# A graph attention layer and a graph convolution on one core: the first layer's opening sums placed by hand, the diagonal loaded once, the adjacency's side sums re-spaced

## The chip, the core and the metric

The kernel runs on one core of one Trainium2 chip. The metric is device time in microseconds (us): the median of three runs. The engines are named as in the profile: PE is TensorE (its weight loads are PEld), DVE is VectorE, ACT is ScalarE, POOL is GpSimd, SP is SyncE, which here only issues DMAs. DMAs are issued from SP's queue and from ACT's queue.

## What is computed

The reference, cut to what matters (N = 3327 nodes, D = 512 features, float32):

```python
h = relu(layernorm(x))
q, k, v = h @ Wq.T + bq, h @ Wk.T + bk, h @ Wv.T + bv
a = q @ k.T / sqrt(D) + adj + adj
x = x + softmax(a) @ v
h = relu(layernorm(x))
A2 = adj + eye(N)
dscale = diagonal(A2) ** -0.5
temp = A2 @ h @ W.T
x = x + relu((dscale[:, None] * A2 * dscale[None, :]) @ temp)
```

## The kernel before

The nodes are padded to 3328, which are 26 tiles of 128. The work has an opening (weights merged, features normalized and transposed, queries projected), then the scores, then the layers.

**The scores.** Four groups of queries (384 or 448 wide) times thirteen pairs of key tiles are 52 score steps. A score step multiplies blocks by a scheme of seven products in the place of eight (`Chain`, L230, used by `Pair.multiply`, L636). PE writes three kinds of PSUM bank, X, Y and Z, two banks of each; DVE evicts each of them into the tile g, which held the adjacency (L646 for a first product, L654 for a later one); ACT takes the exponential of g (L649, L656); the exponentials P and their side sums, which the same scheme needs later, go to DRAM (pd). For the adjacency the first two of four side sums are made here too, by `sum_of_adjacency` (L621: the add at L628, the diagonal's add at L632), and go to DRAM as sumd. What runs beside the products is listed by hand in `beside_of` (L769): a tuple of seven places, called after the seven evictions of a step. `at_score` holds what is issued ahead of a given score step; `fetch(k + 2)` loads the g tiles of the step after the next (L604).

**The layers.** There are three large products: P times h (g = 0), A2 times the second h (g = 1), A2 times temp (g = 2). Each is split twice by the seven-product scheme. The outer split gives seven block products in the order of `ORDER` (L30: p5, p1, p6, p7, p2, p3, p4), each over two strips s (448 and 384 columns in a matmul), each over six pairs of row tiles and a last single tile. These are 3 x 7 x 2 x 7 = 294 steps, numbered k. A step loads its left block (`left`, L984, called by `Step.load`, tile `part`, issued three steps ahead, five slots), makes four sums on DVE (`four_sums`, L162: one of 896 columns at L164, two of 448 at L165 and L166, made two steps ahead, three slots), and multiplies (`Step.multiply`, seven matmuls at L1036, four at L1027 in the last single step). One matmul leaves two records in the profile. The right blocks (`Right`, L706, tile `b`) are loaded five steps and made three steps ahead, once for both strips; for p6 this takes two further 512-wide operations (L743, L744) and loads of 768 KB a step. After a strip the seven PSUM banks are evicted by `Gather` (L1048).

**Beside the layers.** `Job` (L1119) makes the two missing side sums of A2: it loads a block of sumd and one of the adjacency (L1129, L1130), adds them on DVE two steps later (L1134, the diagonal at L1136), and stores the sum to sumd by ACT's queue a step after that (`post`, L957, and `deliver`). There are 52 jobs. They take their tiles from `job_ring` (L973), four slots, two for a job. In the step `prepare` (L892) stands for, the value weights, their bias and the adjacency's diagonal dg are loaded; `load_diagonal` (L899) loads the diagonal again in a second layout, by_32, with 32 partitions to a block; `prepared` (L909) and `scales` (L905) turn both into dscale. `totals`, `place_totals`, `judge` and `judged` handle the row sums of the softmax.

**What sets the order.** Within the scores the order of DVE, PE, POOL and SP is that in which the code issues (`in_order`, L797), and within the layers that of all five queues (L1470). Across the two the scheduler is free. At L1364 to 1371 the code issues, between the two blocks, the first three steps' loads and the first two steps' sums; the third step's sums are issued in the layers' first step. All of these the scheduler moved up into the last score steps. In the layers, a table `between` maps a step to what is issued in it, loads first and the rest after the step's matmuls; `at(k, what)` enters it.

Of the kernel before, what the change touches and what calls it, by code (L numbers as in the profile page):

```python
# [15 lines left out]
P = 128  # L16
# [19 lines left out]
HALF = 13  # L36
# [11 lines left out]
def graph_layers_kernel(  # L48
# [98 lines left out]
    by_32 = const.tile([P, NP // 32], F32, name="by_32")  # L147

# [460 lines left out]
    class Pair:  # L609
# [26 lines left out]
        def multiply(self, qt):  # L636
# [16 lines left out]
            def more(n, ps):  # L653
                nc.vector.tensor_add(a[n], a[n], ps[:, :wd])  # L654
                if n == 1:
                    nc.scalar.activation(g[0], g[0], AF.Exp)  # L656
                beside[{0: 2, 1: 5, 3: 6}[n]]()
# [103 lines left out]
    pairs = {}  # L761
    fours = mid(12, [P, 2, Q[0]], "s4")
    steps = [(n, t) for n in range(len(groups)) for t in range(HALF)]

    def fetch(k):
        if k < len(steps):
            pairs[k] = Pair(*steps[k])

    def beside_of(k):  # L769
        def on(j, what, *args):  # L770
            if 0 <= j < len(steps):
                getattr(pairs[j], what)(*args)

        def difference():
            if k < len(steps) and steps[k][1] >= 6:
                next(more_of, None)

        return (
            lambda: (on(k - 2, "s4"), on(k - 2, "gather", 0)),
            lambda: (on(k - 1, "s3"), on(k - 2, "gather", 1)),  # L780
            lambda: on(k + 1, "sum_of_adjacency", 0),
            lambda: on(k + 1, "sum_of_adjacency", 1),
            lambda: (on(k - 2, "total", 0), difference()),
            lambda: (on(k - 2, "total", 1), on(k - 1, "s1"), next(ahead, None) if k in making else None),
            lambda: (on(k - 1, "s2"), next(ahead, None) if k in making else None),
        )

    coming = queries(0)
    for ins in more_queries(0, coming):
        if ins:  # L790
            after(ins, parts_made[-1])
    for k in range(2):
        fetch(k)
    for m in range(2):
        pairs[0].sum_of_adjacency(m)
    more_of = iter(())
    with in_order(*(e.engine for e in (nc.vector, nc.tensor, nc.gpsimd, nc.sync))):  # L797
        for k, (n, t) in enumerate(steps):
            for what in at_score.get(k, ()):
                what()  # L800
            if t == 0:
                qt = coming
            fetch(k + 2)
            if t == 2 and n + 1 < len(groups):
                coming = queries(n + 1)
                more_of = more_queries(n + 1, coming)
            beside = beside_of(k)
            pairs[k].multiply(qt)
        k = len(steps)
        beside = beside_of(k)  # L810
        for what in beside[:2]:
            what()
        Chain.finish()
        for what in (*beside[5:], *beside_of(k + 1)[:2]):
            what()
        for _ in ahead:
            pass

    def totals():
        for m in range(2):  # L820
            pairs[len(steps_of_scores) - 1].total(m)
        for s in range(2):
            y0, y1 = (by_32[:, 4 * (STRIPS[s] + y * HT[s]) : 4 * (STRIPS[s] + (y + 1) * HT[s])] for y in range(2))
            nc.vector.tensor_sub(y0, y0, y1)

    def place_totals():
        tiled = job_ring([P, P], "tiled")
        for k in range(P // 32):
            nc.vector.tensor_reduce(tiled[:, 32 * k : 32 * k + 32], ident.rearrange("p (a e) -> p e a", e=32), axis=AX.X, op=ALU.add)
        ps = bank(ROLE["p8"], "tot")[:, : 4 * NT]  # L830
        nc.tensor.matmul(ps, tiled, by_32, start=True, stop=True)
        ps = ps.rearrange("p (i a) -> p i a", a=4)
        for a in range(4):
            nc.scalar.copy(tot[32 * a : 32 * a + 32, :], ps[32 * a : 32 * a + 32, :, a])

    steps_of_scores = steps

    ROLE = {"p1": 0, "p6": 2, "p7": 4, "p5": 6, "p2": 7, "p3": 1, "p4": 5, "p8": 3}  # L840

    def banks_for(*names):
        return {r: bank(ROLE[r], r) for r in names}

    verdict = []

    def judge():

        if N < NP:
            other = small.tile([P, 1], F32, name="other")  # L850
            nc.vector.tensor_sub(other, tot[:, NT - 2 : NT - 1], tot[:, NT - 1 :])
            nc.vector.scalar_tensor_tensor(tot[:, NT - 1 :], other, padding, tot[:, NT - 1 :], op0=ALU.mult, op1=ALU.add)
        within = small.tile([P, NT], F32, name="within")
        nc.vector.tensor_scalar(within, tot, SMALL, None, op0=ALU.is_ge)
        good = small.tile([P, NT], F32, name="good")
        nc.vector.scalar_tensor_tensor(good, tot, LARGE, within, op0=ALU.is_le, op1=ALU.mult)
        most = small.tile([P, 2], F32, name="most")
        nc.vector.tensor_reduce(most[:, 0:1], tot, axis=AX.X, op=ALU.max)
        nc.vector.tensor_reduce(most[:, 1:2], tot, axis=AX.X, op=ALU.min)
        ps = bank(ROLE["p8"], "p8")  # L860
        nc.tensor.matmul(ps[:1, :NT], ones, good, start=True, stop=True)
        for k in range(2):
            nc.tensor.transpose(ps[:1, (k + 1) * P : (k + 2) * P], most[:, k : k + 1], ident)
        verdict.append(ps)

    def judged():
        ps, one = verdict[0], small.tile([1, 4], F32, name="one")
        nc.vector.reduce_sum(one[:, 0:1], ps[:1, :NT], axis=AX.X)
        nc.vector.tensor_reduce(one[:, 1:2], ps[:1, P : 2 * P], axis=AX.X, op=ALU.max)
        nc.vector.tensor_reduce(one[:, 2:3], ps[:1, 2 * P : 3 * P], axis=AX.X, op=ALU.min)  # L870

        nc.vector.scalar_tensor_tensor(one[:, 3:4], one[:, 2:3], RATIO, one[:, 1:2], op0=ALU.mult, op1=ALU.is_ge)
        nc.vector.scalar_tensor_tensor(one[:, 3:4], one[:, 0:1], NT * P - 0.5, one[:, 3:4], op0=ALU.is_ge, op1=ALU.mult)
        nc.vector.tensor_scalar(bad, one[:, 3:4], 0.5, None, op0=ALU.is_lt)

    sd = const.tile([P, NT], F32, name="sd")
    rs = const.tile([P, NT], F32, name="rs")

    def weights(src):

        w = [half(k, [P, 2, D], "w") for k in (12, 13)]
        for c in range(DC):
            nc.sync.dma_start(w[c // 2][:, c % 2], src[c * P : (c + 1) * P])
        return [w[c // 2][:, c % 2] for c in range(DC)]

    LD = adjT.shape[1]
    mh = const.tile([P, NT], F32, name="mh")
    nc.vector.memset(mh, -0.5)
    dg = const.tile([P, NT], F32, name="dg")
    bvs = []  # L890

    def prepare():  # L892
        wv_w1.append(weights(wvT))
        bvs.append(half(11, [P, D], "bv_sb"))
        nc.sync.dma_start(bvs[0], bass.AP(tensor=bv.tensor, offset=bv.offset, ap=[[0, P], [1, D]]))
        with nc.allow_non_contiguous_dma(reason="the diagonal, once"):
            nc.sync.dma_start(dg, bass.AP(tensor=adjT.tensor, offset=adjT.offset, ap=[[LD + 1, P], [P * (LD + 1), NT]]))

    def load_diagonal():  # L899
        with nc.allow_non_contiguous_dma(reason="the diagonal, once"):  # L900
            for a in range(4):
                nc.sync.dma_start(by_32[32 * a : 32 * a + 32], bass.AP(tensor=adjT.tensor, offset=adjT.offset,
                                                                      ap=[[LD + 1, 32], [32 * (LD + 1), 4 * NT]]))

    def scales():  # L905
        nc.vector.tensor_scalar(by_32, by_32, 1.0, None, op0=ALU.add)
        nc.gpsimd.tensor_tensor(by_32, by_32, mhalf.to_broadcast(by_32.shape), op=ALU.pow)

    def prepared():  # L909
        nc.vector.reciprocal(rs, tot)  # L910
        nc.vector.tensor_scalar(dg, dg, 1.0, None, op0=ALU.add)
        nc.gpsimd.tensor_tensor(sd, dg, mh, op=ALU.pow)
        nc.scalar.mul(nsd, sd, -1.0)

    wv_w1 = []

    W, differences = [], []

    def other_weights():

        b11, b21, b22, t1, t2, t3 = blocks((11, 12, 13), "w1")
        b12, t4 = (mid(k, [P, 2, E], "w1") for k in (10, 11))
        W.extend((b11, b12, b21, b22, t1, t2, t3, t4))
        for z in range(2):
            for y in range(2):
                block = w1T[z * E : (z + 1) * E, y * E : (y + 1) * E]
# [3 lines left out]
    def difference():  # L930
        next(differences[0])
# [924 lines left out]
```

## Time and profile before

| what | value |
|---|---|
| three runs | 2151.62, 2150.45, 2151.60 us; median 2151.6 |
| profiled execution, its own time | 2150.57 us |
| its span, from first to last instruction | 2148.6 us |
| granted TensorE clock | 1.0 |
| DMA moved | 592.10 MB, mean 276 GB/s |
| first layer matmul | 608.8 us; the scores end near 622 us |
| packets of q1 (SP) and q10 (ACT) | 75.2% and 7.3% of the 16 DMA engines' span |

A row of the profile's timeline gives the start, the duration, the engine, the line, the operation and its tiles, and in brackets the idle time of the engine just before it and what ended it. A row of the view by stretches gives, for each engine, its busy time within the stretch. A row of the view of waits gives the total, the count and the longest. "Landing" is the time at which a DMA's data has arrived.

### The profile page before, as it was taken

The page shows a single profiled execution, that of the slowest core. Times are in us where ns is not written, and L with a number is a line of the kernel's source. Part 1 is how long each engine was busy: PE and PEld are TensorE (multiplying, and loading weights), DVE is VectorE, ACT ScalarE, POOL GpSimd, SP SyncE. Part 2 cuts the span into 40 slices and gives each one's busy share as a digit, 9 for nine tenths or more (in the row PEclk, how much of TensorE's full clock was granted, in tenths as well). Part 3 has the DMA queues.
Part 4 walks back from the last instruction along what each step waited for, and adds up shares of the span by engine and source line. Part 5 has one row for each costly group of instructions (what it writes and reads, how often), then busy time and mean ns, then how long its engine had stood idle before and what let it go on. Part 6 is the DMA issues. An engine that isn't in the chain of part 4 may idle for free.

```text
span 2148.6 us, 20900 instructions
## 1 busy us (share of the span) xinstructions
PE 2137.7 (99%) x6272; PEld 1181.0 (55%) x6272; DVE 1654.2 (77%) x3235; ACT 273.9 (13%) x441; POOL 69.3 (3%) x63
## 2 busy tenths in 40 slices
PE   9999999999999999999999999999999999999998
PEld 6455555555555555555454555555666665555554
DVE  7479888888997688776777778787466666788888
ACT  6312221112110000001111000000111100000000
POOL 2100000000004000000111000000000000000000
PEclk9999999999999999999999999999999999999999
DMA  8678888888999899888787889986646578978997
GB/s 286 230 250 295 302 309 285 305 293 284 329 330 295 292 367 340 285 298 303 263 307 264 300 282 365 322 315 225 195 157 211 155 210 255 303 225 248 267 284 191
DMA packets 402498, 592.10 MB, mean 276 GB/s; under 512 B 139964, under 2 KB 273480, under 8 KB 402376
## 3 DMA queue, kind: packets, MB, share of 16 engines
q1 hardware_dynamic: 374056, 532.72, 75.2%
q10 hardware_dynamic: 28320, 57.95, 7.3%
q8 instruction: 52, 0.85, 0.2%
q14 instruction: 70, 0.57, 0.1%
HBM read 422.71 MB, written 173.87 MB: 278 GB/s over the span
## 4 chain that ended last, share of the span: by engine, by line
PE 97%; DVE 2%; DMA 1%; issue 0%; ACT 0%; POOL 0%; SPq 0%; DVEq 0%; ACTq 0%
PE p L1036 56%; PE Y L642 13%; PE Z L642 7%; PE p L1027 5%; PE p L1143 4%; PE pw L1204 4%; PE X L642 3%; PE Y L440 2%; PE Z L440 1%; PE mm L482 1%; PE X L440 0%; PE tp L320 0%; DVE part L164 0%; DMA qd<-qs 0%; DMA sum<-o 0%
## 5 line engine op out<-in xcount | busy, mean ns | idle before, releaser
L1036 PE MATMUL p<-part,b 128*128 128x448 f32 (+1 forms) x3528 | 1258.0, 513 | 0.3 <-DVE part L1099 0.2
L1036 PEld LDWEIGHTS p<-part,b 128*128 128x128 f32 x3528 | 669.7, 190 | 541.9 <-issue 289.3
L164 DVE TENSOR_TENSOR part<-part 128x896 f32<-128x896 f32 (+1 forms) x252 | 257.0, 1020 | 67.5 <-PE p L1036 29.9
L642 PE MATMUL Y<-qt,hp 128*128 128x448 f32 (+1 forms) x832 | 308.5, 513 | 0.3 <-DVE g L646 0.2
L642 PEld LDWEIGHTS Y<-qt,hp 128*128 128x128 f32 x832 | 157.7, 190 | 134.2 <-issue 72.8
L642 PE MATMUL Z<-qt,hp 128*128 128x384 f32 (+1 forms) x416 | 162.2, 512 | 0.0
L166 DVE TENSOR_TENSOR part<-part,part 128x448 f32<-128x448 f32 (+1 forms) x219 | 129.5, 591 | 15.3 <-PE p L1036 0.5
L165 DVE TENSOR_TENSOR part<-part,part 128x448 f32<-128x448 f32 (+1 forms) x219 | 129.4, 591 | 7.3
L1027 PE MATMUL p<-part,b 128*128 128x448 f32 (+1 forms) x336 | 124.2, 512 | 0.0
L642 PEld LDWEIGHTS Z<-qt,hp 128*128 128x128 f32 x416 | 79.0, 190 | 66.2 <-issue 37.9
L646 DVE SCALAR_TENSOR_TENSOR g<-g,Y 128x384 f32<-128x384 f32 (+1 forms) x156 | 91.6, 587 | 30.2 <-PE Y L642 26.3
L1079 ACT COPY part<-p 128x384 f32<-128x384 f32 (+1 forms) x33 | 16.6, 503 | 655.2 <-PE p L1036 554.8
L1027 PEld LDWEIGHTS p<-part,b 128*128 128x128 f32 x336 | 63.8, 190 | 54.1 <-issue 31.2
L649 ACT ACTIVATE g<-g 128x768 f32<-128x768 f32 (+1 forms) x48 | 43.0, 896 | 346.5 <-DVE g L646 271.8
L642 PE MATMUL X<-qt,hp 128*128 128x384 f32 (+1 forms) x208 | 81.1, 512 | 0.0
L1080 DVE TENSOR_TENSOR part<-p,part 128x384 f32<-128x384 f32 (+1 forms) x33 | 19.3, 586 | 64.1 <-PE p L1036 63.4
L1143 PE MATMUL p<-w,ct 128*128 128x512 f32 x136 | 61.6, 592 | 0.0
L642 PEld LDWEIGHTS X<-qt,hp 128*128 128x128 f32 x208 | 39.5, 190 | 33.1 <-issue 19.3
L199 POOL TENSOR_TENSOR rstd<-ve,mhalf 128x1 f32<-128x1 f32 x46 | 39.5, 862 | 537.7 <-DVE ve L197 528.7
L1099 DVE TENSOR_TENSOR ct<-p,part 128x448 f32<-128x448 f32 (+1 forms) x72 | 42.3, 609 | 16.1 <-PE p L1027 12.1
L1204 PE MATMUL pw<-w,rows 128*128 128x256 f32 x208 | 53.4, 379 | 0.0
L1134 DVE TENSOR_TENSOR job<-job 128x896 f32<-128x896 f32 (+1 forms) x52 | 53.0, 1019 | 0.0
(193 smaller groups left out, 1682.1 us busy)
## 6 DMA issues: line engine op xcount, KB each, us to landing
part<-sum SPq DMA_DIRECT2D x104, 448.0 KB, 4.6
part<-p SPq DMA_DIRECT2D x91, 448.0 KB, 5.9
part<-sum SPq DMA_DIRECT2D x104, 384.0 KB, 4.0
part<-p SPq DMA_DIRECT2D x91, 384.0 KB, 4.4
part<-in_adjT_dram SPq DMA_DIRECT2D x78, 448.0 KB, 5.0
b<-row SPq DMA_DIRECT2D x234, 128.0 KB, 4.8
part<-in_adjT_dram SPq DMA_DIRECT2D x78, 384.0 KB, 3.8
g<-in_adjT_dram SPq DMA_DIRECT2D x52, 448.0 KB, 4.2
```

Of the source, the lines that this page charges most:

```text
L164: yield nc.vector.tensor_add(o[:, 0:2], g[:, 0:4:3], g[:, 1:2].to_broadcast([P, 2, g.shape[-1]]))
L165: yield nc.vector.tensor_add(o[:, 2], o[:, 1], g[:, 0])
L166: yield nc.vector.tensor_add(o[:, 3], o[:, 2], g[:, 2])
L440: nc.tensor.matmul(ps[:, :w], M[B[name]][:, c, o * P : (o + 1) * P], hp[k][:, A[name], c], start=start and c == 0, stop=c == 1, skip_group ...
L642: nc.tensor.matmul(ps[:, :wd], h_of(self.t, name, k), qt[B[name]][:, k], start=start and k == 0, stop=k == 1, skip_group_check=True)
L646: nc.vector.scalar_tensor_tensor(a[n], a[n], 2.0, ps[:, :wd], op0=ALU.mult, op1=ALU.add if sign > 0 else ALU.subtract)
L649: nc.scalar.activation(g[1], g[1], AF.Exp, **({"bias": pad} if self.t == HALF - 1 else {}))
L1027: yield nc.tensor.matmul(ps[("p2", "p3", "p4", "p8")[k]][:, :w], b[:, z], a[:, 0, y], start=k == 3 and not self.seeded, stop=True, skip_gr ...
L1036: yield nc.tensor.matmul(ps[r][:, :w], b[:, i], m, start=self.t == 0 and not adds, stop=self.t == PAIRS - 1 and r in ("p1", "p5", "p6", "p ...
L1134: nc.vector.tensor_add(self.a, self.a, self.b)
L1143: nc.tensor.matmul(ps, cts[s][y][d][:, k * P : (k + 1) * P], w[d], start=d == 0, stop=d == DC - 1)
L1204: nc.tensor.matmul(ps, a, W[B[name]][:, c], start=new and c == 0, stop=c == 1, skip_group_check=True)
```

## The change

- **Opening sums.** The first three layer steps (now `openers`) are loaded ahead of score steps 44, 45 and 46, within the scores' order. The six adds that make the sums of the first two stand at six named places (`opens`): after the fifth eviction of score steps 47 to 50 (one add each), and after the third and fourth of score step 51. The third step's sums stay where they were issued. `parts`, `view`, `turns`, `left`, `Step` and what they need move up in the file unchanged.
- **The diagonal.** It is loaded once, into dg, by ACT's queue ahead of score step 20, behind the exponential issued last. The loads into by_32, its add and its power are gone; in layer step 12 sixteen copies on ACT write by_32 from dscale in the first layout.
- **Small moves.** The value weights and bias are loaded in step 64 and not in step 2. The identity's tiling on DVE is issued in step 2, its matmul stays in step 3. The matmuls of `judge` go from step 8 to 9, `judged` from 9 to 10.
- **The side sums.** The 52 jobs were three steps apart. Now each step has a weight after the loads of the step five ahead (0.5 in the second strip, 0 to 0.3 in the first, 0 in that of p6), and a job is placed when the weights since the last add up to one, at least two steps apart. The jobs start at steps 7, 9, 12, 16, 18, 20, 22, 31, 33, 35, 39, 44, 46, 48, 51, 54, 58, 60, 62, 64, 67, 70, 73, 75, 77, 81, 86, 88, 90, 92, 99, 102, 104, 106, 109, 112, 115, 117, 119, 128, 130, 132, 134, 141, 144, 146, 148, 151, 154, 157, 159, 161.

```diff
-                    nc.scalar.activation(g[0], g[0], AF.Exp)
+                    Pair.exp = nc.scalar.activation(g[0], g[0], AF.Exp)
...
+    openers = [Step(0, ORDER[0], 0, t, right) for t, right in enumerate(ahead_of)]
+    for n, step in enumerate(openers):
+        at_score.setdefault(44 + n, []).append(step.load)
+
+    def sums_of_openers():
+        for step in openers[:2]:
+            yield from step.sums()
+
+    opens, opening = ((47, 4), (48, 4), (49, 4), (50, 4), (51, 2), (51, 3)), sums_of_openers()
...
+    def load_diagonal():
+        step = adjT.shape[1] + 1
+        with nc.allow_non_contiguous_dma(reason="the diagonal, once"):
+            after(nc.scalar.dma_start(dg, bass.AP(tensor=adjT.tensor, offset=adjT.offset, ap=[[step, P], [P * step, NT]])), Pair.exp)
+
+    at_score.setdefault(20, []).append(load_diagonal)
...
+        def open_up(j):
+            if (k, j) in opens:
+                next(opening)
+
...
-            lambda: on(k + 1, "sum_of_adjacency", 0),
-            lambda: on(k + 1, "sum_of_adjacency", 1),
-            lambda: (on(k - 2, "total", 0), difference()),
+            lambda: (on(k + 1, "sum_of_adjacency", 0), open_up(2)),
+            lambda: (on(k + 1, "sum_of_adjacency", 1), open_up(3)),
+            lambda: (on(k - 2, "total", 0), difference(), open_up(4)),
...
-        with nc.allow_non_contiguous_dma(reason="the diagonal, once"):
-            nc.sync.dma_start(dg, bass.AP(tensor=adjT.tensor, offset=adjT.offset, ap=[[LD + 1, P], [P * (LD + 1), NT]]))
-
-    def load_diagonal():
-        with nc.allow_non_contiguous_dma(reason="the diagonal, once"):
-            for a in range(4):
-                nc.sync.dma_start(by_32[32 * a : 32 * a + 32], bass.AP(tensor=adjT.tensor, offset=adjT.offset,
-                                                                      ap=[[LD + 1, 32], [32 * (LD + 1), 4 * NT]]))
-
-    def scales():
-        nc.vector.tensor_scalar(by_32, by_32, 1.0, None, op0=ALU.add)
-        nc.gpsimd.tensor_tensor(by_32, by_32, mhalf.to_broadcast(by_32.shape), op=ALU.pow)
+
+    def place_scales():
+        for a in range(4):
+            to = by_32[32 * a : 32 * a + 32].rearrange("p (i b) -> p b i", b=4)
+            for b in range(4):
+                nc.scalar.copy(to[:, b], sd[32 * b : 32 * b + 32])
...
-    for n, job in enumerate(jobs):
-        k = k0 + n * (k1 - k0) // len(jobs)
-        at(k, job.load)
-        at(k + 2, job.make)
+
+    def jobs_a_step(k):
+
+        ahead = k + 5
+        r, s = ORDER[ahead // (2 * len(every)) % len(ORDER)], ahead // len(every) % 2
+        if k < number_of(0, 0, 1, 0):
+            return 0.0
+        return 0.5 if s else {"p6": 0.0, "p1": 0.3, "p2": 0.3, "p3": 0.3}.get(r, 0.15)
+
+    due, total, placed = 0.0, sum(jobs_a_step(k) for k in range(k0, k1)), []
+    for k in range(k0, k1):
+        due += jobs_a_step(k) * len(jobs) / total
+        if due > 1e-6 and len(placed) < len(jobs) and (not placed or k > placed[-1] + 1):
+            job = jobs[len(placed)]
+            at(k, job.load)
+            at(k + 2, job.make)
+            placed, due = placed + [k], due - 1.0
+    assert len(placed) == len(jobs)
...
-    for k, what in ((1, totals), (3, place_totals), (2, prepare), (6, prepared), (5, load_diagonal), (11, scales), (8, judge), (9, judged)):
+    for k, what in ((1, totals), (2, tile_identity), (3, place_totals), (6, prepared), (8, judge), (9, judge_sums), (10, judged),
+                    (12, place_scales), (number_of(0, 4, 1, 1), prepare)):
         at(k, what)
...
-    for k in range(3):
-        steps[k].load()
...
-    for k in range(2):
-        for _ in steps[k].sums():
-            pass
```

## The prediction

> **What bounds the kernel now.** I read the page first, then TensorE's waits, then the stages around the change by stretches, and last the timeline at each place where TensorE stood.
>
> ```profile
> span 2148.6 us, 20900 instructions
> PE 2137.7 (99%) x6272; PEld 1181.0 (55%) x6272; DVE 1654.2 (77%) x3235; ACT 273.9 (13%) x441; POOL 69.3 (3%) x63
> ...
> PE 97%; DVE 2%; DMA 1%; issue 0%; ACT 0%; POOL 0%; SPq 0%; DVEq 0%; ACTq 0%
> ```
>
> TensorE (PE) is busy for 99% of the span. A rule speaks against resting on that: the Trainium skill, Perfetto Trace Analysis, section "Identifying the Most-Contended Engine", calls matmul busy time a bad measure because matmuls are pipelined, and would judge by the weight loads' share, here 55%. By that rule 45% of the span could be headroom. The timeline decides: in the layers a record of 448 columns starts 375 or 376 ns after the one before, one of 384 columns 322 ns, stage after stage, and only about 30 of 6,272 starts stand out by more than 80 ns. So I count a loss as the excess of a start-to-start distance over that. By this count PE loses 4.6 us in the first 70 us, 2.0 us from 70 to 570 us (nearly all at 75 us, in the projections), 1.4 us from 570 to 625 us, and 3.3 us afterwards; its last record ends at 2142.2 us, and a tail of 6.4 us follows. The order of instructions up to about 545 us (the diagonal's new load aside) and that of the tail are the same in both built programs. What comes after 570 us can give back 1.4 + 3.3 = 4.7 us at most.
>
> ```profile
> 570.00:622.00 52.00, 51.66 (x158) 29.46 (x157) 48.90 (x107) 9.79 (x12) 0.00 (x0) 1.00 0.95 338
> 622.00:685.00 63.00, 63.00 (x185) 33.97 (x184) 47.46 (x105) 2.87 (x8) 17.73 (x2) 1.00 0.96 278
> 750.00:815.00 65.00, 64.90 (x187) 35.07 (x186) 55.38 (x101) 2.99 (x6) 0.00 (x0) 1.00 1.01 370
> ```
>
> Columns: length, then PE, weight loads, DVE, ACT, POOL busy, clock, DMA share, GB/s. First row, end of the scores: DVE 48.9 of 52 us. Second, opening of the layers, where both diagonal loads are: PE lost nothing. Third, p6 of the first product: DMA full.
>
> **Part 1, the opening sums.** Before, the scheduler put the first three steps' sums where it liked among VectorE's (DVE) work on the scores:
>
> ```profile
> 588.38 0.62 DVE L166 TENSOR_TENSOR part<-part,part 128x448 f32<-128x448 f32 x1
> 588.91 0.29 DVE L632 TENSOR_TENSOR o<-o,ident 128x128 f32<-128x128 f32 x1
> ...
> 589.11 0.55 DVE L646 SCALAR_TENSOR_TENSOR g<-g,Y 128x384 f32<-128x384 f32 x1
> ...
> 589.72 0.94 PEld L642 LDWEIGHTS Y<-qt,hp 128*128 128x128 f32 x4 [0.54 <-DVE g L646]
> ```
>
> A sum and a diagonal add stand ahead of the eviction that frees a Y bank, and PE waits. Four such adds (588.4, 590.0, 599.1, 607.8) stand ahead of a Y eviction; the first three of them, with small losses at 620 and 623, make the 1.4 us. Does the change place them better? Only in part. In the built program the first two steps' six adds (1.09 + 0.62 + 0.62 us each step) are behind evictions, but the third step's sums are still free for the scheduler, and five adds stand ahead of a Y eviction: its 896-wide one in one score step, its two 448-wide ones in the next, step 1's two in the last. DVE's work is the same: fifteen 384-wide operations starting some 0.466 us apart are 7.0 us of the 9.03 us of a score step, and two crowded steps carry about 3.2 and 3.5 us more, where before three in a row carried 2.4, 3.0 and 3.2. Less backlog, five places instead of four: 0.7 to 2.0 us, I take 1.2, a gain of 0.2. The adds have two bounds: none ahead of an eviction costs (gain 1.4), or all five at the dearest place's price (599.1: 0.49 us) and a like sum for their backlog, 5 us (loss 3.6).
>
> The loads of these steps also go earlier, two of 448 KB in each of score steps 44 to 46 ahead of the g loads, where before one a step went behind. On SP's queue the g load behind them waited anyway: SP stood 3.9 us ahead of it (548.1 to 552.0). What is left is 0.45 MB more in flight, at the 393 GB/s of full slices 1.2 us; g lands 2.1 to 2.5 us ahead of its first use there (557.1 against 559.7). Cost nothing; without that cover 1.2 us a step, three times.
>
> **Part 2, the diagonal.** Removed: 4 loads into the second layout (SP 8.8 us at L902), an add (0.21), a POOL power (16.96 us). This is what the loads do, from 633 to 656 us in slices of 0.58 us:
>
> ```profile
> DMA  9999999942197999997899999397949966999599
> GB/s 334 289 356 419 378 269 107 62 42 2 1 119 243 339 385 391 337 337 230 358 390 323 93 8 4 2 9 5 7 3 7 10 4 5 10 8 96 166 385 406
> ```
>
> The first dip is the 3,328 four-byte packets of dg (2 to 3 us), the second the 13,312 of the second layout: 13 slices, 7.5 us, of DMA that carries almost nothing. DVE felt the first (2.74 us of waiting for a part load, until 644.4), PE did not: the sums of that step were ready at 646.6 and needed at 655.6. So the removal is worth nothing on PE's path.
>
> Added: dg's load on ACT's queue in score step 20. A rule again speaks against the change: the Trainium skill, DMA: Bandwidth & Descriptors, section "Issuing engines are not separate DMA queues", says that DMAs of all issuing engines interleave on the same 16 DMA engines, so that another queue saves only issue time. By it the g loads of that moment lose the 2 to 3 us all the same. By the trace it costs nothing: the exponential ahead of it ran at 300.2; the g load before it landed at 300.7 and was first used at 305.9, the next was issued at 305.6 for a use at 316.4: 5 us of cover and more. By the rule without that cover it would be 3 us once. ACT spends 0.65 us on the issue (as SP at 632.6); the exponentials queued behind it find ACT idle for some 7 us before each pair. Sixteen copies of 32x26 for the second layout: by the four alike at L834 (171 to 174 ns), 2.8 us on ACT, behind step 12's first eviction; queued behind are job stores and an eviction of step 19, 35 us later. Nothing; exposed, 2.8 us.
>
> **Part 3, small moves.** The value weights and bias (5 DMAs, 1.25 MB, 3.1 us of SP issue, about 3.3 us of DMA) go from step 2 to step 64, at 918 us, where DMA is at 0.78 of full and step 68's sums are 8.5 us early; first use is step 79, at 987 us. Tiling the identity a step earlier puts 1.2 us of DVE before step 5's sums, which were 7 us early, and takes a stall of about 0.1 us from PE. Judging's matmuls a step later than their operands: 0.1 us at 664.3 goes. Together a gain of 0.1.
>
> **Part 4, A2's side sums.** 52 jobs stood every third step. Where p6's blocks are made this is too much for DVE: a step of 5.26 us needs 2.33 (sums) + 1.44 (L743, L744) + 1.15 (four differences) = 4.9, and a job adds 1.09 + 0.29, over 5.26 even when spread over three steps:
>
> ```profile
> 774.48 1.09 DVE L1134 TENSOR_TENSOR job<-job 128x896 f32<-128x896 f32 x1
> 775.49 1.08 DVE L164 TENSOR_TENSOR part<-part 128x896 f32<-128x896 f32 x1
> 776.61 0.63 DVE L165 TENSOR_TENSOR part<-part,part 128x448 f32<-128x448 f32 x1
> 777.28 0.30 PEld L1036 LDWEIGHTS p<-part,b 128*128 128x128 f32 x2 [0.82 <-DVE part L165]
> ```
>
> PE lost 0.37 us here and 0.10 us at 1316.8. At 1128.4 a job at 1124.9 is ahead of the bank evictions: 0.42 us. By the new list loads stand at steps 22, 31, 33, 35 instead of 25, 28, 31, 34, at 121, 128, 130 instead of 124, 127, 130, and no job is made at 96: all three losses, 0.9 us, go. In exchange jobs stand two steps apart elsewhere, 1.4 us of DVE each where sums were 3.5 us or more early; they fit.
>
> **Sum.** 0.2 + 0.1 + 0.9 = 1.2 us. Against the profiled execution (2150.57, span 2148.6 and 2.0 around it) that is 2149.4; the median of the runs is 1.0 higher: 2150.4.
>
> **The rivals.** Less than 0.2% from before, 4.3 us, is about what a measurement of this kernel can tell from no change.
> - *Slower: the jobs' slots.* Four slots hold two jobs. A job's life from load to landed store is 15 to 27 us, median 22.5, outside 985 to 1222 us (there 30 to 46). At three steps apart a slot is wanted again after six, about 29 us; in 15 places of the new list after four, 18 to 21 us. So SP will wait 2 to 5 us for the store, and behind it stand the part loads of four steps ahead and the row loads. Already before: `sum<-job` held SP's job load 6 times, at most 4.0 us. Against it: from landing to PE's need those steps have 7 us or more (step 39: 3.5 + 4.2; step 136: 4.2 + 3.0), the 30 to 46 us lives are where the loads are 24 us early. It decides from a life of 26 us; at 28 half of the places lose about 1.3 us: 10 us, 2160.
> - *The opening gets worse:* all five adds cost: 2150.4 + 3.8 = 2154.2, still within.
> - *Faster by over 0.2%:* all 4.7 us would have to go, 2146.9; but 1.2 us of it (1573 to 1692 us) lies in the weights' products, which the change does not touch, so 2148.1 is the best case.
>
> **Numbers.** Within 0.2%: 0.75, centred at 2150.4, own range 2148.2 to 2154.5. Slower, nearly all by the slots: 0.22. Faster: 0.03. The range goes from 2148.2 into the slot case, to 2157.5; the rest of that case is left out.
>
> **What would show it.** Right: one dip of 4-byte packets near 301 us and none at 645; no PE loss near 776, 1128 and 1317 us; still about 1 us near 590 to 620 us, ahead of Y evictions; more SP waits for `sum<-job`, up to 5 us, without PE losses after them. Wrong: PE losses in steps 35 to 40, 62 to 68, 119 to 138, with DVE waiting for part loads (slots); DVE waits for g near 545 to 570 us (loads ahead); a span under 2146 us.

## The result, and the profile after

The changed kernel takes 2155.02 us (median of 13 runs, 2153.41 to 2157.22), the kernel before 2151.10 us on the same chip (13 runs, 2148.66 to 2153.42): a ratio of 1.0019, 95% interval 1.0011 to 1.0026. That is 3.9 us slower. The prediction was 2150.4, within 0.2% but on the better side of before; the time lies inside its range, where the first rival was. The profiled execution took 2154.96 us, 4.4 more than before's.

The page of the changed kernel, its lines for span, busy time and the chain by engines:

```profile
span 2153.2 us, 20872 instructions
...
PE 2137.6 (99%) x6272; PEld 1181.0 (55%) x6272; DVE 1654.9 (77%) x3234; ACT 277.7 (13%) x457; POOL 52.4 (2%) x62
...
PE 95%; DMA 2%; DVE 2%; issue 0%; SPq 0%; ACT 0%; POOL 0%; DVEq 0%; ACTq 0%
```

PE's work is the same, the span is 4.6 us longer, and PE's share of the chain is 95% where it was 97%. The same three stretches as in the prediction (length, then busy PE, weight loads, DVE, ACT, POOL, clock, DMA share, GB/s):

```profile
570.00:622.00 52.00, 52.00 (x162) 30.19 (x160) 49.85 (x108) 10.01 (x12) 0.00 (x0) 1.00 0.94 327
622.00:685.00 63.00, 61.52 (x182) 33.38 (x181) 46.97 (x104) 6.50 (x24) 5.13 (x1) 1.00 0.77 267
750.00:815.00 65.00, 63.19 (x181) 34.03 (x180) 55.95 (x103) 2.99 (x6) 0.00 (x0) 1.00 0.95 350
```

PE, idle for 0.34 us in the first stretch before, now is not; it idles 1.5 us in the second and 1.8 us in the third. Counted as in the prediction, as the excess of start-to-start distances, here for all kernels of this study (us; a column is named by about where the loss lies in the span; only excesses over 25 ns; the kernels other than before and after are those of the experiments below):

| kernel | 0–570 | 570–626 | 750 | 777 | 946 | 1023 | 1128 | 1317 | 1357 | rest | span |
|---|---|---|---|---|---|---|---|---|---|---|---|
| before | 6.3 | 1.36 | 0 | 0.37 | 0 | 0 | 0.42 | 0.10 | 0 | 1.4 | 2148.6 |
| after | 6.2 | 1.75 | 2.08 | 0 | 0.41 | 0 | 0 | 0 | 2.50 | 1.4 | 2153.2 |
| before, new places | 5.8 | 0.83 | 1.94 | 0 | 0 | 0 | 0 | 0 | 2.38 | 1.4 | 2151.4 |
| after, old places | 6.4 | 1.75 | 0 | 0 | 0 | 0 | 0.42 | 0.71 | 0 | 1.4 | 2149.8 |
| after, six tiles | 5.6 | 1.75 | 0 | 0 | 0 | 0 | 0 | 0 | 0 | 1.8 | 2148.3 |
| after, POOL stores | 5.8 | 1.75 | 0.18 | 0 | 0 | 0 | 0 | 0 | 0 | 1.4 | 2148.3 |
| after, made a step earlier | 5.1 | 1.75 | 0 | 0 | 0 | 1.32 | 0 | 0 | 0 | 1.4 | 2148.6 |
| after, sums held | 6.2 | 0.16 | 1.93 | 0 | 0.18 | 0 | 0 | 0 | 2.50 | 1.4 | 2151.4 |
| after, sums earlier | 4.6 | 0.87 | 2.64 | 0 | 0.21 | 0 | 0 | 0 | 2.40 | 1.6 | 2151.5 |
| all mended | 5.6 | 0.16 | 0 | 0 | 0 | 0 | 0 | 0 | 0 | 1.3 | 2146.2 |
| before, POOL stores | 6.8 | 1.39 | 0 | 0 | 0 | 0 | 0.41 | 0 | 0 | 1.6 | 2149.7 |
| mended, old places | 6.1 | 0.16 | 0 | 0 | 0 | 0 | 0.41 | 0 | 0 | 1.4 | 2147.5 |

Change to after: 0.4 us more at the opening, 0.9 us gone at 777, 1128 and 1317 us, and 5.0 us new at three places that the prediction did not name. At the first of them PE stands in step 28, the first of p6. The timeline, with what VectorE does ahead of PE's wait:

```profile
746.79 1.09 DVE L165 TENSOR_TENSOR part<-part 128x896 f32<-128x896 f32 x1 [5.71 <-DMA part<-p]
...
749.19 0.55 DVE L1099 TENSOR_TENSOR ct<-p,ct 128x384 f32<-128x384 f32 x1
...
751.37 0.68 DVE L744 TENSOR_TENSOR b<-b,rows 128x512 f32<-128x512 f32 x1
...
753.75 1.95 DVE L1118 TENSOR_TENSOR ct<-p,ct 128x384 f32<-128x384 f32 x4
...
754.36 2.90 PE L833 MATMUL p<-part,b 128*128 128x448 f32 x7 [1.81 <-DVE ct L1118]
```

PE waits for the banks that L1118 evicts. Ahead of that DVE has the strip's first evictions (L1099) and the making of a p6 block (L744 on), and all of it stood behind step 28's sums, for which DVE had waited 5.71 us: the `part` load was late. SP's queue ahead of it:

```profile
727.20 0.32 SPq L1148 DMA_DIRECT2D job<-sum  x1
727.57 0.42 SPq L1149 DMA_DIRECT2D job<-in_adjT_dram  x1
728.09 0.86 SPq L789 DMA_DIRECT2D part<-p  x2
729.00 0.91 SPq L721 DMA_DIRECT2D rows<-row  x2
729.95 0.95 SPq L721 DMA_DIRECT2D b<-row  x2
731.74 0.32 SPq L789 DMA_DIRECT2D part<-p  x1
737.59 0.80 SPq L721 DMA_DIRECT2D rows<-row  x2
738.48 0.85 SPq L721 DMA_DIRECT2D b<-row  x2
739.44 1.33 SPq L789 DMA_DIRECT2D part<-p  x2
```

Two gaps: 5.7 us ahead of 727.20, and 5.5 us ahead of 737.59. The last row, 739.44, is the load of step 28; in the kernel before it was issued by 736.7, here by 740.8. What SP waited for a job's store, from 716 to 748 us (total, count, longest), here:

```profile
SPq L721 <- DMA sum<-job: 6.2, 2, 5.5
SPq L1148 <- DMA sum<-job: 5.7, 1, 5.7
```

and in the kernel before, where a row load waits and no job's load does:

```profile
SPq L720 <- DMA sum<-job: 3.6, 1, 3.6
```

The second line of after is the rival's wait: job 6 wants the tiles of job 4, whose store has not landed. The first is another: a row load that shares neither tile nor data with any job waits for a job's store. The trace tells why, by the number of the semaphore that each DMA counts up when it lands (its landing number):

```
issued  queue  what         number   landed
730.20  ACT    sum<-job     100      737.6
737.59  SP     rows<-row    100
724.69  ACT    sum<-job     107      727.2
729.95  SP     b<-row       107
```

The first pair made the wait: the row load's own instruction waits for number 100, which it is itself to count up. In the second pair the store had landed in time.

All DMAs of SP's and ACT's queues together carry eight such numbers (100, 102, 104 to 109), dealt in turn in the program's order, and a DMA is issued only when the one dealt its number before has landed: of the 1,351 pairs in this trace whose first landing is known, none goes against it. So a store that stands early in the program but is issued late, because DVE makes its data late, holds a load some eight DMAs behind it, and everything behind that on SP.

The diagonal, from 633 to 656 us in slices of 0.58 us:

```profile
DMA  9983100057997000048898300008799400008799
GB/s 387 283 310 134 32 21 0 0 85 192 390 369 315 16 0 0 0 59 224 342 267 331 144 0 0 0 0 123 289 395 363 182 16 0 0 0 134 192 358 411
```

The long dips of four-byte packets are gone; where DMA and GB/s are both zero, no packet was under way. The load of dg, now ahead of score step 20, has its four-byte packets from 303 to 307 us, and PE has no excess over 25 ns between 78 and 620 us.

### The profile page after: what moved, and what is told of

Its sections match the earlier page's. It is cut to its first block, busy times and chain, and to the rows that moved or that the text cites. A ratio compares the mean times of both kernels' runs of the same rounds, so it can differ in the third digit from the quotient of the medians.

```text
span 2153.2 us, 20872 instructions
## 1 busy us (share of the span) xinstructions
PE 2137.6 (99%) x6272; PEld 1181.0 (55%) x6272; DVE 1654.9 (77%) x3234; ACT 277.7 (13%) x457; POOL 52.4 (2%) x62
## 4 chain that ended last, share of the span: by engine, by line
PE 95%; DMA 2%; DVE 2%; issue 0%; SPq 0%; ACT 0%; POOL 0%; DVEq 0%; ACTq 0%
PE p L833 55%; PE Y L643 13%; PE Z L643 7%; PE p L824 5%; PE p L1162 4%; PE pw L1223 4%; PE X L643 3%; PE Y L441 2%; DMA part<-p 1%; PE Z L441 1%; PE mm L483 1%; PE X L441 0%; PE tp L321 0%; DMA part<-sum 0%; DVE part L165 0%
## 5 line engine op out<-in xcount | busy, mean ns | idle before, releaser
L1099 DVE TENSOR_TENSOR part<-p,part 128x384 f32<-128x384 f32 (+1 forms) x33 | 19.3, 586 | 62.4 <-PE p L833 61.7
L1118 DVE TENSOR_TENSOR ct<-p,part 128x448 f32<-128x448 f32 (+1 forms) x72 | 42.3, 609 | 17.5 <-PE p L824 13.3
```

## The experiments

The ratio is always to the kernel before, run on the same chip. Three theories of the 5 us: *tiles* (a job's load waits for its tiles), *numbers* (a load waits for its landing number), and that the new places are not the cause at all.

**Only the new places, and all but the new places.** The lists of steps are exchanged between the two kernels, nothing else:

```diff
-        k = k0 + n * (k1 - k0) // len(jobs)
+    for k in range(k0, k1):
+        due += jobs_a_step(k) * len(jobs) / total
...
```

> The kernel before with only the new places of the side sums. If the places are the cause (theory slots: a job's load waits for a tile that the store of two jobs earlier still holds, with all later loads queued behind it; or theory numbers: a load waits because its completion number was last dealt to a job's store, which is issued late), the new losses of TensorE at about 750, 945 and 1357 us come here too, some 4 to 5 us, the old ones at 777, 1128 and 1317 us (0.9 us) go, and the time is about 2155 us. If the opening or the diagonal were the cause it stays at 2151 us.

Measured: 2154.59 us, ratio 1.0017 (1.0010 to 1.0024).

> The changed kernel with the side sums back at every third step. Either theory of the side sums: the 4.9 us of TensorE loss at 750, 945 and 1357 us go and about 0.9 us come back, with the opening's 1.8 us kept: about 2151.3 us. If the opening or the single layout of the diagonal were the cause: 2155 us.

Measured: 2151.58 us, ratio 1.0001 (0.9993 to 1.0009). The places are the cause of the loss, 3.2 of the 3.9 us between the medians; openers, diagonal and small moves together cost nothing that can be measured. The loss at 946 us does not come with the places alone; the weights' five loads, now in step 64, stand there on SP between two job loads (922.3 to 924.6 us) and may be what is missing; that was not tried.

**Six tiles.** Jobs take a third pair of tiles where two spare ones are free:

```diff
+    job_ring6 = ring(*spare, (half, 14))
...
-            self.a, self.b = (job_ring([P, H[0]], "job")[:, :w] for _ in range(2))
+            take = job_ring6 if now[0] < 72 or 112 <= now[0] < 140 else job_ring
+            self.a, self.b = (take([P, H[0]], "job")[:, :w] for _ in range(2))
```

> The changed kernel with six job tiles in place of four in steps 7 to 71 and 112 to 139. Theory slots: SP's waits of 5.7, 5.1 and 7.1 us at a job's own load go, and the time falls by 4 us to about 2151 us. Theory numbers: those waits go, but the row loads behind still wait for a store's landing (5.5, 4.8 and 4.7 us), the layer's part is issued less than 1 us earlier, and the time stays between 2154 and 2155.5 us.

Measured: 2150.32 us, ratio 0.9996 (0.9987 to 1.0004). The tiles' theory holds here; that of the numbers alone, by which the time should have stayed at 2154 or more, does not.

**Stores on POOL's queue.** Only the queue of the jobs' stores changes. POOL's DMAs carry eight numbers of their own (111 to 118):

```diff
-            post(sumd[self.s][self.j][:, 2 + self.k], self.a)
+            posted.append((now[0], lambda: nc.gpsimd.dma_start(sumd[self.s][self.j][:, 2 + self.k], self.a)))
```

> The changed kernel with the side sums' stores issued from GpSimd's queue in place of ScalarE's; its transfers are dealt completion numbers of their own, so no load of SP shares one with a job's store, while four tiles stay. Theory numbers: SP's waits of row and part loads for a job's store go, TensorE's losses at 750, 945 and 1357 us shrink to under 1.5 us together, about 2151.5 us. Theory slots: the waits at a job's own load stay (5 to 7 us each) and the time stays at 2155 us, or goes up if GpSimd's stores land later.

Measured: 2149.91 us, ratio 0.9993 (0.9984 to 1.0001). By the tiles' theory this should have changed nothing. SP's waits from 716 to 748 us, in this kernel:

```profile
SPq L1148 <- DMA sum<-job: 6.2, 1, 6.2
...
SPq L721 <- DMA t<-b: 3.7, 1, 3.7
```

(the second stands at 748 us, behind the loads of step 28) and in the one with six tiles:

```profile
SPq L721 <- DMA rows<-row: 3.7, 5, 1.7
...
SPq L789 <- DMA sum<-job: 2.6, 2, 1.6
```

With POOL's stores the wait for the tiles is still whole, 6.2 us, and only that for the number is gone. With six tiles the wait for the tiles is gone, and SP, 6 us earlier, meets the numbers at a better time: 1.6 us at most for a store's. Either cure suffices. The wait for the tiles alone (POOL's stores) cost PE 0.18 us here, the wait for the number alone (before, 3.6 us in the same stretch) nothing; the two in a row cost 2.1. A wait of 5.5 us for the number alone was not tried. Over the whole span the kernel with POOL's stores waits even longer for tiles than after (below), and PE loses no more than that:

```profile
SPq L1148 <- DMA sum<-job: 96.6, 24, 9.8
```

How much waiting a step can bear shows in the time from the end of its sums to PE's first matmul of it. In steps 28 and 140, the first of p6 and of the second product's p7, that is 3.8 and 3.7 us before, 0.9 and 0.5 after, 5.8 and 8.3 with six tiles, 2.8 and 3.4 with POOL's stores. In step 28 PE loses nothing at 3.8, 0.18 us at 2.8 and 2.1 us at 0.9.

**Made a step earlier.** `at(k + 2, job.make)` becomes `at(k + 1, job.make)`.

> The changed kernel with each side sum made one step after its load in place of two, so that its store is issued and lands about 5 us earlier. If the stores' lateness is the cause, through tiles or through completion numbers, both waits shrink (a life of 19 to 20 us in place of 25), TensorE's losses at 750, 945 and 1357 us fall under 1 us, and the time is about 2151 us. If VectorE now waits for the job's own load (landed 5 to 9 us after issue), up to 1 us of that comes back.

Measured: 2152.39 us, ratio 1.0002 (0.9994 to 1.0011). The losses at 750, 946 and 1357 us are gone, and SP's waits at a job's own load are 5.8 us in all, where after had 82.7. In exchange there is one new loss, of another kind than expected:

```profile
1018.13 0.95 DVE L1153 TENSOR_TENSOR job<-job 128x768 f32<-128x768 f32 x1
1019.12 0.29 DVE L1155 TENSOR_TENSOR job<-job,ident 128x128 f32<-128x128 f32 x1
...
1021.91 1.94 DVE L1118 TENSOR_TENSOR part<-p,part 128x384 f32<-128x384 f32 x4
...
1023.23 2.15 PE L833 MATMUL p<-part,b 128*128 128x448 f32 x5 [1.05 <-ACT p L1092]
```

A job fell into the turn of a strip, ahead of the evictions that free the banks, beside the attention's row work. DVE works without a gap up to the evictions: it is not a wait for a load but DVE's order.

**The opening.** After's end of the scores:

```profile
620.38 1.09 DVE L165 TENSOR_TENSOR part<-part 128x896 f32<-128x896 f32 x1
...
623.26 0.55 DVE L647 SCALAR_TENSOR_TENSOR g<-g,Y 128x384 f32<-128x384 f32 x1
...
623.86 0.64 PE L833 MATMUL p<-part,b 128*128 128x448 f32 x1 [1.48 <-DVE g L647]
```

PE waits for the last Y eviction, and the first sum of step 3, which nothing pins, stands ahead of it. Two kernels were run for this. In one, the sums of steps 2 and 3 are held behind it:

```diff
+                if (self.g, self.r, self.s) == (0, ORDER[0], 0) and self.t in (2, 3):
+                    after(ins, Pair.out)
```

> The changed kernel with the sums of steps 2 and 3 of the layer held behind the scores' last eviction. If the 1.75 us that TensorE loses at 622 us come from step 3's first sum (1.09 us) standing ahead of that eviction, 0.66 us or less are left and the time is about 2153.9 us. If they come from the two sums pinned into the last score step (1.24 us), which stay, the loss stays near 1.7 us and the time at 2155 us.

Measured: 2154.49 us, ratio 1.0016 (1.0010 to 1.0023). In the other the pinned places are (46, 4), (47, 4), (48, 4), (49, 4), (50, 2), (50, 4):

> The changed kernel with the six pinned sums one score step earlier (steps 46 to 50 in place of 47 to 51), so that the last score step has none. VectorE's order then also has step 3's first sum behind the last eviction. The loss at 622 us goes whole (0 to 0.3 us left), the time is about 2153.4 us. If new losses come at 570 to 605 us, where VectorE has the least room, they are the three of before (0.3 to 0.6 us each).

Measured: 2155.94 us, ratio 1.0019 (1.0010 to 1.0028). In the traces the loss of 1.75 us falls to 0.16 us where the sums are held, and to 0.87 us where they are earlier, of which 0.57 us now lie at 606 to 609 us, one score step before. Held:

```profile
620.14 6.18 PE L836 MATMUL p<-part,b 128*128 128x448 f32 x16
...
621.08 0.54 DVE L647 SCALAR_TENSOR_TENSOR g<-g,Y 128x384 f32<-128x384 f32 x1
...
621.54 1.08 DVE L165 TENSOR_TENSOR part<-part 128x896 f32<-128x896 f32 x1
```

The eviction now stands ahead of the sum, and PE runs through. By the runs' times neither kernel can be told from after; the opening is known from the traces only.

**All mends, with the new and with the old places.** Six tiles, POOL's stores, sums held and earlier; then the same with the jobs at every third step:

> The changed kernel with all mends together: six tiles, stores on GpSimd's queue, pinned sums one step earlier, sums of steps 2 and 3 held. Losses left: about 4.2 and 1.9 us up to 570 us, 0 to 0.3 us at the opening, 2.3 us behind; 1.7 us less than with GpSimd's stores alone (2149.9 us): about 2148.3 us. If a loss only moves, 2149.5 us or more.

Measured: 2149.02 us, ratio 0.9991 (0.9984 to 0.9998).

> All mends (six tiles, GpSimd's stores, sums earlier and held) with the side sums at every third step as before. If the new places are worth what the prediction gave them, this is 0.9 us slower than with the new places (2149.0 us): 2149.9 us, with losses at 777, 1128 and 1317 us. If the mends cure those losses too, it is 2149.0 us and the new places are worth nothing.

Measured: 2149.15 us, ratio 0.9993 (0.9984 to 1.0001). With all mends and the new places the kernel beats both, before by 2.1 us. The two lists differ by 0.13 us in the medians, less than can be told, and in the traces by the 0.41 us at 1128.

**Before, with POOL's stores.**

> The kernel before with only the side sums' stores moved to GpSimd's queue; the old places and the old opening stay. In the kernel before, SP's row loads wait 22.9 us in ten waits for a job's store, and TensorE loses 0.9 us at 777, 1128 and 1317 us. If those losses hang on the completion numbers, they go and the time is about 2150.2 us; if they come from VectorE's own order (a side sum made in a step with no room), they stay and so does the time, 2151.1 us.

Measured: 2150.81 us, ratio 0.9999 (0.9991 to 1.0007). In the trace the losses at 777 and 1317 us are gone, that at 1128 us stays. The runs' times cannot tell so small a gain.

## Why the prediction was wrong, by its steps

- *PE bounds, losses are counted by starts:* right. The differences of the spans, 7 us at most, are found again as such losses to within 0.9 us, and in the mended kernel those behind 570 us are down from 3.6 to 1.5 us (excesses over 25 ns).
- *Part 1, opening:* taken at 1.2 us of loss within 0.7 to 2.0; it is 1.75. The mechanism was named (adds ahead of a Y eviction); the early losses at 589 to 600 us went, and one larger came at the end. The term mis-sized is the backlog of the last score step: two pinned sums (1.24 us) and a free one (1.09 us) meet there. The free one is step 3's first sum; the prediction counted the free sums of step 2, in other score steps, and not this one.
- *Loads ahead, part 2:* right. Up to 570 us the losses are as before (6.2 us against 6.3), and with the old places the change as a whole is at 1.0001. The 3 us that the prediction drew from the rule on queues as the price of the diagonal's load without cover did not come. For the jobs' stores that rule (the Trainium skill, DMA: Bandwidth & Descriptors, "Issuing engines are not separate DMA queues": another engine saves only the time to initiate the DMA) is too strong for this program: moving them to POOL's queue gained 5.1 us between the medians (ratios to before 1.0019 and 0.9993), though they were issued later there, because it took them out of the numbers that the loads share.
- *Part 3, gain of 0.1:* not seen. The judging's stall stayed (0.09 us at 669), an excess of 0.04 us at 642 went, and the weights' loads stand ahead of where the 0.41 us at 946 us came up; whether they are its cause is open.
- *Part 4, what goes:* right, all 0.9 us went. But the reason given, too much work for DVE in p6, was only half of it. Before with POOL's stores has the same DVE work in the same places, and two of the three losses are gone: there p6's loads, held up by the stores' numbers, came too late for DVE to catch up. Small shifts decide these two: after with the old places loses nothing at 777 us and 0.71 us at 1317. Only the one at 1128 us, which stays in both of these kernels, is DVE's order.
- *Part 4, "they fit":* **this step failed.** The jobs two steps apart were charged to DVE, where sums were 3.5 us or more early, and put at nothing. They cost on SP, and through it 4.3 us of PE with the new places alone and 5.0 us in after. SP's waits for `sum<-job` at a job's own load rose from 6 times and 14.8 us before

```profile
SPq L720 <- DMA sum<-job: 22.9, 10, 5.6
...
SPq L1129 <- DMA sum<-job: 14.8, 6, 4.0
```

to 19 times and 82.7 us after (the lines of L720 and L721 are row loads):

```profile
SPq L1148 <- DMA sum<-job: 82.7, 19, 9.6
...
SPq L721 <- DMA sum<-job: 24.1, 8, 5.5
```

- *The rival of the slots:* half of the mechanism, given 0.22. Three things in its price were off. It priced the waits at 2 to 5 us and had them decide from a life of 26 us: the tile that SP waited for ahead of step 28 was held by a job of 24.9 us, the one ahead of step 140 by a job of 26.3 us, and the longest of the 19 waits is 9.6 us. It left out the second wait, for the number, which was in before's view already (the row loads above); the two add up on one queue, 5.7 + 5.5 us at 737, 5.1 + 4.8 us at 921 to 931, and 7.1 + 4.7 us at 1343. And the cover was read at the wrong end: from landing to PE's first matmul step 28 had 7.7 us, but behind its sums stand the strip's evictions and a p6 block, so that the 3.8 us from the end of the sums are what counts. Its steps were 35 to 40, 62 to 68 and 119 to 138; it was the first step of a strip, 28, 70 and 140, each behind a run of jobs two apart.

The Trainium skill, Perfetto Trace Analysis, section "Identifying Dependency Chains", tells one to look at the semaphores an instruction waits for. The prediction read only the name of the other DMA; the number of the semaphore in the trace would have shown that a load can wait for a transfer it has nothing to do with.

Open: the 1128 us loss was not taken apart further, and the parts of the weights' loads and of the jobs in the 0.41 us at 946 us were not tried singly.

## What to carry to other kernels

A queue that issues in order adds up its waits: price a new wait together with those already there, and against the thinnest cover behind it, which is where evictions and other work queue behind the awaited operation, not where the awaited data is first multiplied. When a load waits for a store it shares no data with, look at the completion semaphores: a store whose data is made late is best issued where it shares none with the loads, or with its data made sooner. When work is moved away from one engine's tight place, see what it does on the queue that feeds the engine.

## What was not expected of the hardware and its program

- Eight landing numbers serve SP's and ACT's queues together; in the changed kernel, from 630 to 1480 us, SP waited about 160 us for the number of its next DMA (38 us of it for jobs' stores) and about 405 us for tiles and data, counting waits over 0.3 us. With POOL's stores the first is about 118 us.
- A job's store (448 KB at most) landed 5.6 us after its issue in the median when POOL issued it; when ACT did, 4.9 us in after (2.3 to 9.4 us) and 5.9 us before, so a difference by queue is not shown. The issue came 1.4 against 1.1 us after the start of the add.
- Nearly the same instructions up to 570 us lost 4.6 to 6.8 us of PE's time in twelve profiles: a spread about half as large as the effect studied.
